# The last chunk of a feature-interaction network done by halves of its columns in two accumulators

**The chip, the cores and the metric.** One core of one Trainium2 chip. The time is that of the device, in microseconds (us), median of several executions.

## The reference

A batch of 1024 samples with 64 features of 16 numbers goes through three layers of a compressed interaction network:

```python
for i in range(n):                                   # n = 3
    z = einsum('bfe,bge->bfge', x0, h)               # all products of features
    y = einsum('oc,bce->boe', Ws[i], z) + bs[i][None, :, None]
    if i != n - 1: x_i, h = y[:, :64], y[:, 64:]     # half is kept, half goes on
    else: x_i = y
    xs.append(x_i)
pooled = sum(concatenate(xs, axis=1), axis=2)
return pooled @ fc_w.T + fc_b                        # one number a sample
```

## The kernel before

The batch is cut into 32 chunks of 512 columns (32 samples by 16 numbers). VectorE makes the products `z` of a chunk, TensorE contracts them with `w_all` in 16 matmuls into one accumulator of 128 x 512:

```python
def contract(c, j):
    for i in range(NI):                              # NI = NJ = 4
        t = j * NI + i
        nc.tensor.matmul(accs[c], w_all[:, t, w_cols(c)], zs[c, j][:, i, :], start=..., stop=...)
```

From chunk 8 on, four chunks make a group. Two kinds of small matmuls are shared by a group, in parts of the array that run side by side: the squares (32 rows of the array for each chunk), and for each pair of chunks two weighted matmuls and two `y` matmuls (a quarter of the array each):

```python
def contract_shared(first):
    for r in range(4):
        c, at = first + r, slice(32 * r, 32 * r + 32)
        nc.tensor.matmul(accs[c], w_sq[at, w_cols(c)], zls[first // 4][at], ..., tile_position=(32 * r, 0))
    for k in (first // 2, first // 2 + 1):
        ...
        for n in range(2):
            c, rows, q = 2 * k + n, halves[n], halves[1 - n]
            nc.tensor.matmul(accs[c][q], v1w[rows], xxs[k][rows], start=False, ...)
        for rows in halves:
            nc.tensor.matmul(ys[k][rows], bd[rows, rows], xxs[k][rows], start=True, stop=True)
```

Behind a chunk's last matmul come a copy on ScalarE and a multiply and a reduction on VectorE. The sums of all chunks are pooled by matmuls with a matrix of ones into `po`, and `finish` sends them out:

```python
def factors(c):
    ...
    nc.scalar.copy(q[h], accs[c][64 - h.start : 128 - h.start])
    nc.vector.scalar_tensor_tensor(uu, accs[c][h], bh1[h], q[h], ALU.add, ALU.mult)
...
# the end; chunk 31 has been contracted in the loop, with pool(first, 1), pool(first, 0)
# in its middle and finish(first) behind it (first: pairs 0 to 14, last: pair 15)
sums(NP - 1, parts=slice(1, 2))
sums(NP - 1, slice(0, 64), slice(0, 1))
pool(last, 1)
factors(NCH - 1)
sums(NP - 1, slice(64, 128), slice(0, 1))
pool(last, 0)
finish(last)
```

Of the kernel before, what the change touches and what calls it, by code (L numbers as in the profile page):

```python
# [32 lines left out]
F32 = mybir.dt.float32  # L36
AF = mybir.ActivationFunctionType
ALU = mybir.AluOpType
# [3 lines left out]
E = 16  # L42
B = 1024
CB = 32
N = CB * E
NCH = B // CB
NI = 4
NJ = 4
# [12 lines left out]
def cin_kernel(ctx, tc, xra, xrb, xh, wh, w0r, w1h, w2t, wx1, wx0, vec, out):  # L61
    nc = tc.nc
# [5 lines left out]
    sp = ctx.enter_context(tc.tile_pool(name="sp", bufs=2))  # L68
    ps = ctx.enter_context(tc.tile_pool(name="ps", bufs=2, space=bass.MemoryType.PSUM))
# [3 lines left out]
    def const_tile(name, shape):  # L73
        return const.tile(shape, F32, tag=name, name=name)

    def z_tile(name):

        return zp.tile([128, NI, N], F32, tag="z", name=name)

# [3 lines left out]
    def set_tile(name):  # L83
        return setup.tile([128, NI * N], F32, tag="set", name=name)

# [3 lines left out]
    fc2, bh1, bh2 = vs[:, 0:1], vs[:, 1:2], vs[0:64, 2:3]  # L89
# [18 lines left out]
    w_all = const_tile("w_all", [128, NT + 1, 192])  # L108
    w_sq = const_tile("w_sq", [128, 192])
    v1w = const_tile("v1w", [128, F])  # L110
# [5 lines left out]
    xas, xbs, zls, xxs = {}, {}, {}, {}  # L116

    def load_xa(c, at=slice(0, NI)):
        if c not in xas or at.start == 0:
            xas[c] = xp.tile([128, NI, N], F32, tag="xa", name=f"xa_{c}")  # L120
        nc.sync.dma_start(
            out=xas[c][:, at, :],
            in_=bass.AP(
                tensor=xra.tensor, offset=c * XR * N + at.start * N,
                ap=[[N, 128], [1, (at.stop - at.start) * N]],
            ),
        )

    def load_chunk(c):
        load_xa(c)  # L130
        xb = xp.tile([128, NJ, N], F32, tag="xb", name=f"xb_{c}")
        nc.sync.dma_start(out=xb, in_=xrb[c])
        xbs[c] = [xb[:, j, :] for j in range(NJ)]
# [20 lines left out]

    acc = const_tile("acc", [128, 2, NCH // 2, CB])
    hb = const_tile("hb", [128, NF, N // 2])
    accs, uus, zs, ys = {}, {}, {}, {}

    def new_acc(c, n=N):
        accs[c] = ps.tile([128, n], F32, tag="acc", name=f"acc_{c}", bufs=4)  # L160

    def product(c, j, pieces=1):
# [10 lines left out]
    def squares(c):  # L173
        zls[c] = xp.tile([128, N], F32, tag="zl", name=f"zl_{c}", bufs=4)
        nc.scalar.activation(zls[c][0:64], xas[c][0:64, 0, :], AF.Square)  # L175
# [16 lines left out]
    def w_cols(c):  # L192
        return slice(64, 192) if c >= FIRST and c % 2 else slice(0, 128)

    def contract(c, j):
        for i in range(NI):
            t = j * NI + i
            nc.tensor.matmul(  # L198
                accs[c], w_all[:, t, w_cols(c)], zs[c, j][:, i, :],
                start=(t == 0 and (c < FIRST or c % 4 < 2)),  # L200
                stop=(t == NT - 1 and c >= FIRST and c % 4 >= 2),
            )
# [4 lines left out]
    def contract_shared(first):  # L207

        for r in range(4):
            c, at = first + r, slice(32 * r, 32 * r + 32)  # L210
            nc.tensor.matmul(  # L211
                accs[c], w_sq[at, w_cols(c)], zls[first // 4][at], start=(r >= 2), stop=(r < 2),
                tile_position=(32 * r, 0),
            )
        for k in (first // 2, first // 2 + 1):
            ys[k] = ps.tile([128, N], F32, tag="y", name=f"y_{k}")
            for n in range(2):
                c, rows, q = 2 * k + n, halves[n], halves[1 - n]
                nc.tensor.matmul(  # L219
                    accs[c][q], v1w[rows], xxs[k][rows], start=False, stop=(c % 4 < 2),  # L220
                    skip_group_check=True,
                )
            for rows in halves:
                nc.tensor.matmul(ys[k][rows], bd[rows, rows], xxs[k][rows], start=True, stop=True)  # L224



    H2 = N // 2

    def half_contract(c, part, j):  # L230

# [2 lines left out]
        for t in (NT,) if j == NJ else range(j * NI, (j + 1) * NI):  # L234
            z = zls[c] if t == NT else zs[c, j][:, t % NI, :]
            for n in range(2):
                nc.tensor.matmul(  # L237
                    accs[c][halves[n]], w_all[rows, t, cols], z[rows, n * H2 : (n + 1) * H2],
                    start=(t == 0), stop=(t == NT),
# [5 lines left out]
    def uu_tile(k):  # L245
        if k not in uus:
            uus[k] = sp.tile([128, 2, N], F32, tag="uu", name=f"uu_{k}")
        return uus[k]

    def factors(c):  # L250

        uu = uu_tile(c // 2)[halves[c % 2], 0, :]
        if c in HEAD:
            for n in range(2):
                at = halves[n]
                nc.vector.tensor_tensor(  # L256
                    uu[:, n * H2 : (n + 1) * H2], accs[c][at], hb[at, HEAD.index(c), :], ALU.mult
                )
            return
        h = halves[c % 2 if c >= FIRST else 0]  # L260
        q = sp.tile([128, N], F32, tag="q", name=f"q_{c}")
        nc.scalar.copy(q[h], accs[c][64 - h.start : 128 - h.start])  # L262
        nc.vector.scalar_tensor_tensor(uu, accs[c][h], bh1[h], q[h], ALU.add, ALU.mult)  # L263

    def v0x(k):
        ys[k] = ps.tile([128, N], F32, tag="y", name=f"y_{k}")
# [2 lines left out]
    def x_v0x(k):  # L269
        nc.vector.scalar_tensor_tensor(uu_tile(k)[:, 1, :], ys[k], cx, xxs[k], ALU.add, ALU.mult)  # L270

    def sums(k, rows=slice(0, 128), parts=slice(0, 2)):

        nc.vector.tensor_reduce(  # L274
            acc[rows, parts, k, :],
            uus[k][rows, parts].rearrange("p k (b e) -> p k b e", e=E),
            AX.X,
            ALU.add,
        )
# [5 lines left out]


    new_acc(c0, H2)
    squares(c0)
    for j in range(NJ):
# [14 lines left out]
    for n in range(2):  # L304
        pv = ps.tile([128, 512], F32, tag="set", name=f"pv2_{n}")
        for k in range(4):
            nc.tensor.matmul(
                pv[32 * k : 32 * k + 32], fv2, w2s[n][:, k * 512 : (k + 1) * 512],
                start=True, stop=True,
                tile_position=(0, 32 * k),  # L310
            )
        nc.scalar.copy(v2r[:, n, :], pv)


    new_acc(c1, H2)
    for j in range(NJ - 1):
        product(c1, j)
# [56 lines left out]
    def head(c):  # L374
        new_acc(c, H2)
        for j in range(NJ):
            product(c, j)
        for j in range(NJ + 1):
            half_contract(c, 0, j)
        keep_h1(c)  # L380
# [29 lines left out]

    new_acc(c4, H2)
    for j in range(NJ - 1):
# [52 lines left out]
    for j in range(2):  # L465
        nc.tensor.matmul(
            pc, fcol[:, j : j + 1].to_broadcast([128, 2]), bcol[:, j : j + 1],
            start=(j == 0), stop=(j == 1),
# [13 lines left out]

    NP = NCH // 2
    po = ps.tile([2, NP, CB], F32, tag="set", name="po")
# [3 lines left out]
    def pool(pairs, part):  # L488
        nc.tensor.matmul(  # L489
            po[:, pairs, :], ones, acc[:, part, pairs, :],  # L490
            start=(part == 1), stop=(part == 0), skip_group_check=True,
        )

    def finish(pairs):
        nc.scalar.activation(res[:, pairs, :], po[:, pairs, :], AF.Identity, bias=cst)  # L495
        nc.scalar.dma_start(out=outs[:, pairs, :], in_=res[:, pairs, :])


    order = list(range(2, NCH))
    first, last = slice(0, NP - 1), slice(NP - 1, NP)  # L500
    for s, c in enumerate(order):
        k, shared = c // 2, c >= FIRST
        if s + 2 < len(order):
            ahead = order[s + 2]
            load_chunk(ahead)
            last_tile(ahead)
            for j in range(NJ):
                product(ahead, j)
        if not shared or c % 4 < 2:
            new_acc(c, H2 if c in HEAD else N)  # L510
        for j in range(NJ):
            if j == 2:
                if s == 0:
                    for n in KEPT:
                        half_contract(n, 1, NJ)
                if s == 1:
                    v0x(0)
                if c % 2 and not shared:
                    v0x(k)
                if s == len(order) - 1:  # L520
                    pool(first, 1)
                    pool(first, 0)
            if c in HEAD:
                half_contract(c, 1, j)
            else:
                contract(c, j)
        if c in HEAD:
            half_contract(c, 1, NJ)
        elif not shared:
            contract_last(c)  # L530
        elif c % 4 == 1:
            for n in (1, 2):
                new_acc(c + n)
            contract_shared(c - 1)
        if s == len(order) - 1:
            finish(first)

        if s == 0:
            for n in KEPT:
                factors(n)  # L540
        elif not shared or c % 4 in (0, 3):
            factors(order[s - 1])
        elif c % 4 == 2:
            factors(c - 2)
            factors(c - 1)
            x_v0x(k - 1)
            x_v0x(k)
        if s == 1:
            x_v0x(0)
            sums(0)  # L550
        if c % 2 and not shared:
            x_v0x(k)
        elif s and c % 2 == 0:
            sums(k - 1)
    sums(NP - 1, parts=slice(1, 2))
    sums(NP - 1, slice(0, 64), slice(0, 1))
    pool(last, 1)
    factors(NCH - 1)
    sums(NP - 1, slice(64, 128), slice(0, 1))
    pool(last, 0)  # L560
    finish(last)

# [71 lines left out]
```

## Time and profile before

| | before |
|---|---|
| time | 501.08 us median of 6 runs, 500.87 to 501.39 |
| TensorE's share of the chain that ended last | 91% |
| from the last group's squares to the end | 37.48 us |
| a group's squares, weighted and `y` matmuls | 2.948 us, in each of the six groups |
| copy, multiply, reduction behind the last matmul | 0.577, 0.757, 0.682 us |

TensorE is busy without a gap from early on, so whatever lengthens its stream lengthens the kernel; only behind the last matmul do the other engines set the time. The lines stand in the prediction.

### The profile page before, as it was taken

To read this page: it belongs to the slowest core of one execution; us is meant where nothing else is said; L and a number is where in the kernel's file an instruction comes from. 1 tells how busy PE (TensorE), PEld (TensorE's weight loads), DVE (VectorE), ACT (ScalarE), POOL (GpSimd) and SP (SyncE) were. 2 spreads that over 40 slices of the span, in tenths; PEclk is the share of its full clock that TensorE was granted. 3 is DMA by queue.
4 is the path that set the end of the run, shared out by engine and by line. 5 is a ranking of instruction groups with operands and counts; after the bars stand their busy time and mean duration, and the time that the engine had idled before them with its cause. 6 is when DMAs were issued, how large, how long until landed. Compare 5 with 4: busy or idle time off the path is not lost.

```text
span 499.2 us, 4338 instructions
## 1 busy us (share of the span) xinstructions
PE 483.8 (97%) x1814; PEld 222.6 (45%) x1814; DVE 381.8 (76%) x233; ACT 92.5 (19%) x159; POOL 1.4 (0%) x14
## 2 busy tenths in 40 slices
PE   3899999999999999999999999999999999999996
PEld 1455654456444344443444434443444434444432
DVE  4999699988999889898777686776877777770302
ACT  1243033122111121312011121111111121010001
POOL 1000000000000000000000000000000000000000
PEclk9999999999999999999999999999999999999999
DMA  8997895353454443446144442333444430000000
GB/s 327 425 419 226 338 421 208 116 230 129 181 235 175 170 174 162 177 175 256 66 169 169 168 168 113 118 136 138 168 169 168 167 131 39 0 0 0 2 0 0
DMA packets 14787, 82.80 MB, mean 166 GB/s; under 512 B 3788, under 2 KB 4460, under 8 KB 5232
## 3 DMA queue, kind: packets, MB, share of 16 engines
q1 hardware_dynamic: 13644, 81.24, 41.5%
q10 hardware_dynamic: 1124, 1.29, 0.9%
q8 instruction: 14, 0.23, 0.2%
q14 instruction: 5, 0.04, 0.0%
HBM read 80.88 MB, written 1.64 MB: 165 GB/s over the span
## 4 chain that ended last, share of the span: by engine, by line
PE 91%; DMA 5%; ACT 1%; ACTq 0%; SPq 0%; DVE 0%; issue 0%
PE acc L198 75%; PE acc L237 11%; DMA w1s<-in_w1h 4%; PE acc L219 2%; DMA xb<-in_xrb 1%; PE acc L211 1%; PE y L267 1%; PE acc L205 1%; PE pm L336 0%; PE po L489 0%; ACT zl L175 0%; ACT zl L181 0%; ACT m_sb L341 0%; ACT xx L190 0%; ACTq L360 0%
## 5 line engine op out<-in xcount | busy, mean ns | idle before, releaser
L198 PE MATMUL acc<-z,w_all 128*128 128x512 f32 x864 | 374.1, 593 | 0.0
L166 DVE TENSOR_TENSOR z<-xa,xb 128x2048 f32<-128x2048 f32 (+1 forms) x141 | 314.9, 2270 | 49.9 <-PE acc L198 39.7
L198 PEld LDWEIGHTS acc<-z,w_all 128*128 128x128 f32 x864 | 163.3, 190 | 208.3 <-issue 207.8
L237 PE MATMUL acc<-z,w_all 128*64 128x256 f32 x640 | 74.7, 389 | 10.4 <-DVE w_all L282 8.4
L171 ACT ACTIVATE z<-xa 32x512 f32<-32x512 f32 x35 | 21.9, 625 | 323.5 <-DVE z L166 320.7
L263 DVE SCALAR_TENSOR_TENSOR uu<-acc,vs,q 64x512 f32<-64x512 f32 x27 | 20.2, 750 | 62.4 <-ACT q L262 62.3
L237 PEld LDWEIGHTS acc<-z,w_all 128*64 128x64 f32 x640 | 45.8, 140 | 39.1 <-DVE w_all L282 9.9
L274 DVE TENSOR_REDUCE acc<-uu 128x64 f32<-128x1024 f32 (+2 forms) x18 | 20.2, 1125 | 0.3
L190 ACT COPY xx<-xa 64x512 f32<-64x512 f32 x32 | 19.6, 613 | 0.4
L262 ACT COPY q<-acc 64x512 f32<-64x512 f32 x27 | 15.7, 580 | 19.3 <-PE y L224 12.9
L186 ACT ACTIVATE sq<-xa 32x512 f32<-32x512 f32 x24 | 15.1, 628 | 0.6
L270 DVE SCALAR_TENSOR_TENSOR uu<-y,cx,xx 128x512 f32<-128x512 f32 x16 | 11.4, 745 | 0.3
L224 PE MATMUL y<-xx,bd 64*64 64x512 f32 x48 | 11.6, 602 | 0.0
L219 PE MATMUL acc<-xx,v1w 64*64 64x512 f32 x48 | 11.6, 602 | 0.0
L211 PE MATMUL acc<-sq,w_sq 32*128 32x512 f32 x48 | 6.8, 640 | 0.0
L175 ACT ACTIVATE zl<-xa 64x512 f32<-64x512 f32 x11 | 6.8, 623 | 0.1
L219 PEld LDWEIGHTS acc<-xx,v1w 64*64 64x64 f32 x48 | 2.8, 132 | 7.9 <-issue 7.9
L237 PE MATMUL acc<-zl,w_all 64*64 64x256 f32 (+1 forms) x40 | 6.1, 393 | 0.0
L243 ACT ACTIVATE hb<-acc,vs 128x256 f32<-128x256 f32 x5 | 2.4, 474 | 20.0 <-PE acc L237 20.0
L495 ACT ACTIVATE res<-po,cst 2x480 f32<-2x480 f32 (+1 forms) x2 | 0.9, 464 | 24.0 <-PE po L489 24.0
L181 ACT COPY zl<-xa 64x512 f32<-64x512 f32 x8 | 4.9, 616 | 0.1
L256 DVE TENSOR_TENSOR uu<-acc,hb 64x256 f32<-64x256 f32 x10 | 4.2, 421 | 0.2
(52 smaller groups left out, 52.0 us busy)
## 6 DMA issues: line engine op xcount, KB each, us to landing
xa<-in_xra SPq DMA_DIRECT2D x34, 1024.0 KB, 4.8
xb<-in_xrb SPq DMA_DIRECT2D x34, 1024.0 KB, 7.0
w<-in_w2t SPq DMA_DIRECT2D x2, 1024.0 KB, 13.5
xa<-in_xra SPq DMA_DIRECT2D x2, 512.0 KB, 4.1
w1s<-in_w1h SPq DMA_DIRECT2D x1, 1024.0 KB, 20.3
w1x<-in_wx SPq DMA_DIRECT2D x1, 1024.0 KB, 8.7
w0x<-in_wx SPq DMA_DIRECT2D x1, 1024.0 KB, 10.3
xb<-in_xrb SPq DMA_DIRECT2D x1, 768.0 KB, 7.0
```

Of the source, the lines that this page charges most:

```text
L166: nc.vector.tensor_tensor(zs[c, j][:, i : i + n, :], xas[c][:, i : i + n, :], xbs[c][j].unsqueeze(1).to_broadcast([128, n, N]), ALU.mult,)
L171: nc.scalar.activation(zs[c, j][SQ, 0, :], xas[c][SQ, 0, :], AF.Square)
L186: nc.scalar.activation(zls[c // 4][at : at + 32], xas[c][0:32, 0, :], AF.Square)
L190: nc.scalar.copy(xxs[c // 2][to], xas[c][to, 0, :])
L198: nc.tensor.matmul(accs[c], w_all[:, t, w_cols(c)], zs[c, j][:, i, :], start=(t == 0 and (c < FIRST or c % 4 < 2)), stop=(t == NT - 1 and ...
L211: nc.tensor.matmul(accs[c], w_sq[at, w_cols(c)], zls[first // 4][at], start=(r >= 2), stop=(r < 2), tile_position=(32 * r, 0),)
L219: nc.tensor.matmul(accs[c][q], v1w[rows], xxs[k][rows], start=False, stop=(c % 4 < 2), skip_group_check=True,)
L224: nc.tensor.matmul(ys[k][rows], bd[rows, rows], xxs[k][rows], start=True, stop=True)
L237: nc.tensor.matmul(accs[c][halves[n]], w_all[rows, t, cols], z[rows, n * H2 : (n + 1) * H2], start=(t == 0), stop=(t == NT),)
L262: nc.scalar.copy(q[h], accs[c][64 - h.start : 128 - h.start])
L263: nc.vector.scalar_tensor_tensor(uu, accs[c][h], bh1[h], q[h], ALU.add, ALU.mult)
L274: nc.vector.tensor_reduce(acc[rows, parts, k, :], uus[k][rows, parts].rearrange("p k (b e) -> p k b e", e=E), AX.X, ALU.add,)
```

## The change

The intent: contract the last chunk's first 256 columns completely, then the second 256 into another accumulator. The first half's copy, multiply and reduction run while TensorE does the second half, and only steps of 256 columns are left behind the last matmul. The core of the diff:

```diff
     def new_acc(c, n=N):
+        if c == NCH - 1:
+            parts[c] = [
+                (ps.tile([128, H2], F32, tag=tag, name=f"acc_{c}_{n}", bufs=bufs), cols)
+                for n, (tag, bufs, cols) in enumerate(
+                    (("acc", 4, slice(0, H2)), ("set", 2, slice(H2, N)))
+                )
+            ]
+            return
... contract, the squares, the weighted matmuls and factors go over the parts of chunk 31 ...
-                if s == len(order) - 1:
-                    pool(first, 1)
-                    pool(first, 0)
...
-        if s == len(order) - 1:
-            finish(first)
...
-    sums(NP - 1, parts=slice(1, 2))
+    sums(NP - 1, of=slice(1, 2))
     sums(NP - 1, slice(0, 64), slice(0, 1))
-    pool(last, 1)
     factors(NCH - 1)
-    sums(NP - 1, slice(64, 128), slice(0, 1))
+    sums(NP - 1, slice(64, 128), slice(0, 1), slice(0, CB // 2))
+    for j in range(NJ):
+        if j == 2:
+            pool(first, 1)
+            pool(first, 0)
+            pool(last, 1)
+        contract(NCH - 1, j, 1)
+    finish(first)
+    factors(NCH - 1, slice(1, 2))
+    sums(NP - 1, slice(64, 128), slice(0, 1), slice(CB // 2, CB))
     pool(last, 0)
     finish(last)
```

More of the change, by code (lines that the diff above doesn't have):

```diff
@@ L45 @@
 N = CB * E
+H2 = N // 2
 NCH = B // CB
@@ L156, in cin_kernel @@
     hb = const_tile("hb", [128, NF, N // 2])
-    accs, uus, zs, ys = {}, {}, {}, {}
+    accs, uus, zs, ys, parts = {}, {}, {}, {}, {}
     def new_acc(c, n=N):
+        if c == NCH - 1:
[6 more added lines that the diff above has]
+            return
         accs[c] = ps.tile([128, n], F32, tag="acc", name=f"acc_{c}", bufs=4)
@@ L193, in w_cols, with pieces, contract @@
         return slice(64, 192) if c >= FIRST and c % 2 else slice(0, 128)
-    def contract(c, j):
+    def pieces(c):
+        return parts[c] if c in parts else [(accs[c], slice(0, N))]
+    def contract(c, j, piece=0):
+        acc_c, cols = pieces(c)[piece]
         for i in range(NI):
@@ L198, in contract @@
             nc.tensor.matmul(
-                accs[c], w_all[:, t, w_cols(c)], zs[c, j][:, i, :],
+                acc_c, w_all[:, t, w_cols(c)], zs[c, j][:, i, cols],
                 start=(t == 0 and (c < FIRST or c % 4 < 2)),
@@ L210, in contract_shared @@
             c, at = first + r, slice(32 * r, 32 * r + 32)
-            nc.tensor.matmul(
-                accs[c], w_sq[at, w_cols(c)], zls[first // 4][at], start=(r >= 2), stop=(r < 2),
-                tile_position=(32 * r, 0),
-            )
+            for acc_c, cols in pieces(c):
+                nc.tensor.matmul(
+                    acc_c, w_sq[at, w_cols(c)], zls[first // 4][at, cols], start=(r >= 2),
+                    stop=(r < 2), tile_position=(32 * r, 0),
+                )
         for k in (first // 2, first // 2 + 1):
@@ L218, in contract_shared @@
                 c, rows, q = 2 * k + n, halves[n], halves[1 - n]
-                nc.tensor.matmul(
-                    accs[c][q], v1w[rows], xxs[k][rows], start=False, stop=(c % 4 < 2),
-                    skip_group_check=True,
-                )
+                for acc_c, cols in pieces(c):
+                    nc.tensor.matmul(
+                        acc_c[q], v1w[rows], xxs[k][rows, cols], start=False, stop=(c % 4 < 2),
+                        skip_group_check=True,
+                    )
             for rows in halves:
                 nc.tensor.matmul(ys[k][rows], bd[rows, rows], xxs[k][rows], start=True, stop=True)
-    H2 = N // 2
     def half_contract(c, part, j):
@@ L248, in uu_tile, with factors @@
         return uus[k]
-    def factors(c):
+    def factors(c, which=slice(0, 1)):
         uu = uu_tile(c // 2)[halves[c % 2], 0, :]
@@ L260, in factors @@
         h = halves[c % 2 if c >= FIRST else 0]
-        q = sp.tile([128, N], F32, tag="q", name=f"q_{c}")
-        nc.scalar.copy(q[h], accs[c][64 - h.start : 128 - h.start])
-        nc.vector.scalar_tensor_tensor(uu, accs[c][h], bh1[h], q[h], ALU.add, ALU.mult)
+        for acc_c, cols in pieces(c)[which]:
+            q = sp.tile([128, N], F32, tag="q", name=f"q_{c}_{cols.start}")
+            nc.scalar.copy(q[h, cols], acc_c[64 - h.start : 128 - h.start])
+            nc.vector.scalar_tensor_tensor(
+                uu[:, cols], acc_c[h], bh1[h], q[h, cols], ALU.add, ALU.mult
+            )
     def v0x(k):
@@ L270, in x_v0x, with sums @@
         nc.vector.scalar_tensor_tensor(uu_tile(k)[:, 1, :], ys[k], cx, xxs[k], ALU.add, ALU.mult)
-    def sums(k, rows=slice(0, 128), parts=slice(0, 2)):
+    def sums(k, rows=slice(0, 128), of=slice(0, 2), half=slice(0, CB)):
         nc.vector.tensor_reduce(
-            acc[rows, parts, k, :],
-            uus[k][rows, parts].rearrange("p k (b e) -> p k b e", e=E),
+            acc[rows, of, k, half],
+            uus[k][rows, of, E * half.start : E * half.stop].rearrange("p k (b e) -> p k b e", e=E),
             AX.X,
```

## The prediction

> **What bounds the kernel now.** I read the page first, parts 1, 2 and 4, to see which engine sets the end; then the chain of work over the last 40 us, to see the order of the end; then the groups by form for the durations; then the engines' own timelines around the places that the change touches.
>
> ```profile
> PE 483.8 (97%) x1814; PEld 222.6 (45%) x1814; DVE 381.8 (76%) x233; ACT 92.5 (19%) x159; POOL 1.4 (0%) x14
> PE   3899999999999999999999999999999999999996
> DVE  4999699988999889898777686776877777770302
> PE 91%; DMA 5%; ACT 1%; ACTq 0%; SPq 0%; DVE 0%; issue 0%
> ```
>
> TensorE is the bound: 91% of the chain that ended last, nines from the third slice to the last but one. Nothing that takes time from VectorE or ScalarE matters except behind the last matmul. The chain there:
>
> ```profile
> 464.78 20.80 PE acc L198 x48
> 485.58 1.70 PE po L489 x4
> 487.28 7.08 PE acc L198 x16
> 494.36 0.02 issue
> 494.38 0.58 ACT q L262
> 494.97 0.03 issue
> 494.99 0.77 DVE uu L263
> 495.76 0.02 issue
> 495.79 0.69 DVE acc L274
> 496.48 0.04 issue
> 496.52 0.23 PE po L489 x2
> 496.76 0.02 issue
> 496.78 0.28 ACT res L495
> ```
>
> One matmul of the program is two instructions in the trace (432 calls of L198 in the code, x864 on the page), so chunk 31 is 32 instructions of 512 columns, split 16 and 16 by the pooling of the first 15 pairs. Behind it stand six steps, 494.36 to 497.06, then the output's DMA (to 499.2). Three of the six, the copy, the multiply and the reduction, have 512 columns: 0.58 + 0.77 + 0.69 = 2.04 us. These are what the change halves. The rest (final pooling, 32-column activation, DMA) has no 512.
>
> The places where the change adds matmuls:
>
> ```profile
> 461.76 1.14 PE L211 MATMUL acc<-sq,w_sq 32*128 32x512 f32 x8
> 462.84 0.65 PE L219 MATMUL acc<-xx,v1w 64*64 64x512 f32 x2
> 462.85 0.65 PE L224 MATMUL y<-xx,bd 64*64 64x512 f32 x2
> 463.32 0.59 PE L219 MATMUL acc<-xx,v1w 64*64 64x512 f32 x2
> 463.33 0.60 PE L224 MATMUL y<-xx,bd 64*64 64x512 f32 x2
> ```
>
> Here several matmuls run at once in different parts of the array: the four calls of one pair (two of L219, two of L224) start together as first passes at 462.84, and their second passes start together 0.48 us later. The trace shows such grouping only where the calls use different parts; the pairs of L237, which come back to the same two parts, run pair by pair, 0.21 us a step.
>
> **What the Trainium skill says.**
> - "TensorE: Matmul & The Clock Gate", Back-to-back issue gap: the warm gap is the columns over the rate plus about 2.5 ns fixed. The trace has the same shape at half that rate: 429 ns for 512 columns (427 at 1.2 columns a ns, and 2). The L237 pairs of 256 columns repeat every 215 to 216 ns. So two of 256 cost about 2 ns more than one of 512.
> - Same page, LDWEIGHTS: a load takes the columns over 1.2, here 107 ns, and can be pulled ahead under the running matmul. The trace agrees: two exposed loads start 108 ns apart; each is recorded as 190 ns and starts 2 ns after the matmul before. 190 is under 213, so under a 256-column matmul it should still be hidden. No 256-column matmul with 128 weight columns is in this trace.
> - Same page, The mechanism: matmuls start in order. It matters below, where a second half needs a part of the array that the first half still uses.
> - "TensorEngine Tiling (Array Packing)", Key Properties: changing the tiling mode drains the array. The trace agrees: going into the pooling the step is 523 ns and not 429, and the first step coming back is 534, so 0.20 us for the round trip. The change keeps one such trip.
>
> **The change part by part.**
> 1. Behind the last matmul. Copy: ScalarE's slope here is (651 - 278) / 448 = 0.83 ns a column (480 and 32 columns of L495); 256 columns fewer are 0.21 us, leaving 0.37. Multiply: VectorE's slope is (1224 - 420) / 768 = 1.05 ns a column (L166 and L282 forms); 0.27 us fewer, leaving 0.49. Reduction: (1215 - 669) / 512 = 1.07; 0.27 us fewer, leaving 0.41. Sum: -0.75 us, all on the path.
> 2. The contraction of chunk 31: 64 instructions of about 215.6 ns = 13.80 us against 32 x 428.9 = 13.72: +0.07 us on the path.
> 3. The last pair's first pooling (two 32-column instructions, 28 ns apart at 494.28) moves from beside the ScalarE copy into the stream: +0.06 us. The first pairs' pooling (1.70 us) only moves from between two quarters to between two eighths: 0.
> 4. The squares' matmul of chunk 31 (L211, its fourth row part) becomes two. The other three parts run their second pass of 427 ns while the fourth does 213, so its second half can start in the free half of that time: its two passes of 213 then end 213 + 213 + 213 = 640 ns after the second passes' start instead of 427, less what goes before the mode switch's drain; taking the load into account I put +0.1 to +0.3 us, middle 0.2.
> 5. The weighted matmul of chunk 31 (L219) becomes two in one part. If the group breaks where a part comes back, the five calls run as {30, 31a} and {31b, y, y}: 31a's second pass ends at 640 ns, then 31b, y and y start, and y's two passes of 427 end at 1494 instead of 854: +0.64 us. If all first passes go before all second passes, in order, y starts behind 31a at 213: +0.21 us. If the parts ran wholly on their own: 0. I take +0.35.
> 6. The output of the first 15 pairs goes from 487.3 to about 490.8 on ScalarE (0.65 us and 0.50 of issue), 3 us before the last copy: 0. The copy of chunk 30, which waited for it until 488.55, moves to about 478.6: nothing waits for it.
> 7. The first half's copy, multiply and reduction run under the second half's matmuls: 485.3 to about 486.7, and the pooling wants them at 488.7 at the earliest: 0.
>
> Sum: -0.75 + 0.07 + 0.06 + 0.2 + 0.35 = -0.07 us; span 499.1, time 501.0. The gain and what it costs are of one size.
>
> **The rivals.**
> - The clean gain: the added matmuls of 4 and 5 fit into the array's free parts. For it: the parts do run side by side (four within 20 ns of each other). Against: starts are in order, and a second half returns to a busy part. It makes -0.75 + 0.13 = -0.62, 500.5 us.
> - The groups break: 4 and 5 at their worst, 0.3 + 0.64. For it: the L237 pairs never mix with the next pair. It makes +0.3, 501.4 us.
> - The weight loads no longer hide under 213 ns. For it: the record says 190 and 23 ns remain; PEld is then nearly always busy. Against: what the array needs is 107. If 20 ns showed on each of 64, +1.3 us: 501.7 to 502.3. I give it one in ten.
> - A wait takes the place: the final pooling or the second accumulator waits. Against: the second accumulator takes a bank whose last user (a constant's set-up) is long done by chunk 8, and the first 15 pairs' output ran at once after its pooling in the kernel before, though later matmuls had been issued, so its wait is exact. A late first output would cost up to 1.2 us; one in twenty.
>
> **Range and chances.** All outcomes worked out lie between 500.5 and 502.3, within 0.3% of 501.09; the three runs of before span 0.2. The likely mass is 500.4 to 501.5. 2% is 10 us, the whole tail behind the last matmul is 5 us, so neither side of 2% has a mechanism.
>
> **What would show it right or wrong.** The chain's end should read about 0.37, 0.49, 0.41 for copy, multiply and reduction; larger values fell step 1. 32 instructions of L198's line with 256 columns should take 6.9 us; 7.5 or more would mean exposed loads (step 2). From the start of the fourth group of squares to the start of chunk 30's contraction the kernel before takes 464.71 - 461.76 = 2.95 us; after, 2.95 would show the clean gain, 3.5 my middle, 3.9 broken groups (steps 4 and 5). An idle stretch of TensorE before the pooling, or the long ScalarE activation behind 494, would show a new wait.

## The result

The changed kernel takes 500.51 us (median of 6 runs, 500.32 to 500.66); before, 501.08. That is 0.57 us less. Ratios are the mean time of one kernel's fast runs over that of the other's of the same rounds, so not quite the ratio of the medians: 0.9989, with a 95% interval of 0.9976 to 1.0001, which just includes 1: the whole time alone does not settle that there is a gain, and the rest rests on the traces.

From the page of the changed kernel, the busy line and the shares of the chain that ended last:

```profile
PE 483.2 (97%) x1850; PEld 229.3 (46%) x1850; DVE 382.3 (77%) x235; ACT 92.7 (19%) x160; POOL 1.4 (0%) x14
PE 91%; DMA 5%; ACT 1%; SPq 0%; ACTq 0%; issue 0%; DVE 0%
```

The bound is the same: TensorE has 91% of the chain. 36 matmul instructions were added: 32 in the contraction, two in the squares and two in the weighted matmuls. The end of the chain that ended last, after (start, duration, what):

```profile
488.98 1.76 PE po L507 x6
490.74 3.67 PE acc L213 x16
...
494.43 0.37 ACT q L278
...
494.82 0.50 DVE uu L279
...
495.35 0.43 DVE acc L292
495.78 0.14 issue
495.91 0.23 PE po L507 x2
```

The three steps read 0.37, 0.50 and 0.43 where they read 0.58, 0.77 and 0.69. One line is new: between the reduction's end and the last pooling there is 0.14 us of "issue" where there was 0.04. (By the single times of the trace, used from here on, the gap is 0.147 us and was 0.056.)

The place where I had expected half the gain to be lost, TensorE's timeline over the last group's weighted and `y` matmuls (start, duration, engine, line, operation, tiles, shapes, count):

```profile
463.60 0.59 PE L236 MATMUL acc<-xx,v1w 64*64 64x512 f32 x2
463.61 0.65 PE L241 MATMUL y<-xx,bd 64*64 64x512 f32 x2
463.82 0.80 PE L236 MATMUL acc<-xx,v1w 64*64 64x256 f32 x3
464.09 0.60 PE L241 MATMUL y<-xx,bd 64*64 64x512 f32 x2
464.25 0.38 PE L236 MATMUL acc<-xx,v1w 64*64 64x256 f32 x1
464.62 0.70 PE L213 MATMUL acc<-z,w_all 128*128 128x512 f32 x1
```

L236 is the weighted matmul, L241 is `y`. The program issues chunk 30's weighted matmul, the two halves of chunk 31's, and then the two `y`. Single starts in the trace: chunk 31's part starts a 256-column pass at 463.606, 463.822, 464.038 and 464.253, every 0.216 us without a gap; the first passes of both `y` start at 463.613 and 463.619, before the second half of chunk 31, which stands ahead of them in the program. The whole group takes 3.004 us instead of 2.948. Almost all of that is in `y`, not in chunk 31's part. Before, the weights of this pair's `y` were loaded while the first pair's matmuls still ran (from 463.331, the matmul at 463.758). Now they are loaded only at 463.610 and 463.617, with the matmuls, and from first to second pass it takes 0.480 us instead of 0.429.

Where the time went, both traces from the start of the last group's squares to the end, 37.483 us before and 37.017 after:

| term | us |
|---|---|
| copy 0.577 to 0.363, multiply 0.757 to 0.491, reduction 0.682 to 0.416 | -0.746 |
| the group's squares (1.071 to 1.076) | +0.005 |
| the group's weighted and `y` matmuls (1.877 to 1.928) | +0.051 |
| the contraction of chunks 30 and 31 (27.932 to 28.012, pooling taken out) | +0.080 |
| pooling in the stream (1.701 to 1.760) | +0.059 |
| from the reduction's end to the last pooling's start (0.056 to 0.147) | +0.091 |
| the rest | -0.006 |
| sum | -0.466 |

The span of the two profiled runs differs by 0.617 us. The other 0.15 lie before the first group's squares (171.37 us into the trace before, 171.22 after), where the two programs are the same. The same changed kernel, run once more in a later job (a set of runs on one chip), began them at 172.05. This part is not the change's.

### The profile page after: what moved, and what is told of

It reads as the page before. It is cut to its first block, busy times and chain, and to the rows that moved or that the text cites. A ratio compares the mean times of both kernels' runs of the same rounds, so it can differ in the third digit from the quotient of the medians.

```text
span 498.6 us, 4414 instructions
## 1 busy us (share of the span) xinstructions
PE 483.2 (97%) x1850; PEld 229.3 (46%) x1850; DVE 382.3 (77%) x235; ACT 92.7 (19%) x160; POOL 1.4 (0%) x14
## 4 chain that ended last, share of the span: by engine, by line
PE 91%; DMA 5%; ACT 1%; SPq 0%; ACTq 0%; issue 0%; DVE 0%
PE acc L213 75%; PE acc L252 11%; DMA w1s<-in_w1h 4%; PE acc L236 2%; DMA xb<-in_xrb 1%; PE acc L227 1%; PE y L285 1%; PE acc L220 1%; PE po L507 0%; PE pm L354 0%; ACT zl L185 0%; ACT zl L191 0%; ACT m_sb L359 0%; ACT xx L200 0%; ACTq L378 0%
## 5 line engine op out<-in xcount | busy, mean ns | idle before, releaser
L213 PE MATMUL acc<-z,w_all 128*128 128x512 f32 (+1 forms) x896 | 374.2, 578 | 0.0
L213 PEld LDWEIGHTS acc<-z,w_all 128*128 128x128 f32 x896 | 169.4, 190 | 202.1 <-issue 200.0
L279 DVE SCALAR_TENSOR_TENSOR uu<-acc,vs,q 64x512 f32<-64x512 f32 (+1 forms) x28 | 20.5, 731 | 61.5 <-ACT q L278 61.3
L278 ACT COPY q<-acc 64x512 f32<-64x512 f32 (+1 forms) x28 | 15.8, 564 | 36.4 <-PE acc L213 22.9
L292 DVE TENSOR_REDUCE acc<-uu 128x64 f32<-128x1024 f32 (+3 forms) x19 | 20.3, 1073 | 0.4
L241 PE MATMUL y<-xx,bd 64*64 64x512 f32 x48 | 11.7, 604 | 0.0
L236 PE MATMUL acc<-xx,v1w 64*64 64x512 f32 (+1 forms) x50 | 11.6, 584 | 0.0
L227 PE MATMUL acc<-sq,w_sq 32*128 32x512 f32 (+1 forms) x50 | 6.8, 620 | 0.0
L236 PEld LDWEIGHTS acc<-xx,v1w 64*64 64x64 f32 x50 | 3.1, 132 | 7.5 <-issue 7.4
L227 PEld LDWEIGHTS acc<-sq,w_sq 32*128 32x128 f32 x50 | 2.2, 183 | 4.6 <-issue 4.5
```

Of the source, the lines that this page charges most:

```text
L213: nc.tensor.matmul(acc_c, w_all[:, t, w_cols(c)], zs[c, j][:, i, cols], start=(t == 0 and (c < FIRST or c % 4 < 2)), stop=(t == NT - 1 and ...
L227: nc.tensor.matmul(acc_c, w_sq[at, w_cols(c)], zls[first // 4][at, cols], start=(r >= 2), stop=(r < 2), tile_position=(32 * r, 0),)
L236: nc.tensor.matmul(acc_c[q], v1w[rows], xxs[k][rows, cols], start=False, stop=(c % 4 < 2), skip_group_check=True,)
L278: nc.scalar.copy(q[h, cols], acc_c[64 - h.start : 128 - h.start])
L279: nc.vector.scalar_tensor_tensor(uu[:, cols], acc_c[h], bh1[h], q[h, cols], ALU.add, ALU.mult)
L292: nc.vector.tensor_reduce(acc[rows, of, k, half], uus[k][rows, of, E * half.start : E * half.stop].rearrange("p k (b e) -> p k b e", e=E), ...
```

## The experiments

The open points: why the halves in the shared matmuls cost almost nothing; whether the gain is that of the tail (the steps behind the last matmul) alone; where the new 0.09 us in front of the last pooling come from; and how far the cut could go. "Stretch" below is the time from the start of the last group's squares to the end of the trace; it is 37.483 us for the kernel before and 37.017 for the changed one. Twelve kernels ran.

**The pooling behind the last matmul.**

```diff
             pool(first, 0)
-            pool(last, 1)
         contract(NCH - 1, j, 1)
     finish(first)
+    pool(last, 1)
```

> The change, with the last pair's first pooling moved from the middle of the second half's matmuls to behind the last one, after the output of the first 15 pairs. Theory (a second wait): in the changed kernel the last pooling is the first writer of that accumulator after ScalarE has read it, so it waits for ScalarE as well as for VectorE, and TensorE spends an extra 51 ns event instruction behind the reduction (gap from the reduction's end to the matmul 147 ns, 56 before the change). With the other pooling taking the wait for ScalarE while the tail's copy runs, the gap should go back to about 56 ns, and the two 32-column matmuls (0.06 us) leave the stream: 0.15 us less than the change, 500.36 by the clock of the changed kernel's 500.51. Rival (the gap comes from somewhere else, the chip's state or the shorter reduction): the gap stays near 147 ns and only 0.06 us goes, 500.45.

Measured: 500.39 us against 501.02 of the kernel before in the same rounds (ratio 0.9987, interval 0.9974 to 0.9999); stretch 36.872, which is 0.145 less than the change. The pooling in the stream is back to 1.70 us. The chain of waits at the end:

```profile
495.27 0.43 DVE acc L292
495.69 0.04 issue
495.74 0.23 PE po L507 x2
```

The gap is back to 0.054 us (0.04 on the chain). The theory of a second wait holds, the rival falls.

**The last pair's pooling in a bank of its own.**

```diff
+    pos = {0: po}
     def pool(pairs, part):
+        if pairs.start not in pos:
+            pos[pairs.start] = ps.tile([2, 1, CB], F32, tag="y", name="po_last")
         nc.tensor.matmul(
-            po[:, pairs, :], ones, acc[:, part, pairs, :], ...
+            po_of(pairs), ones, acc[:, part, pairs, :], ...      # finish reads po_of(pairs) too
```

> The change, with the last pair's two poolings in a bank of their own, at the same places in the program. Theory (a second wait): nothing of the last pooling's accumulator is read by ScalarE before, so only the wait for VectorE is left: gap from reduction to matmul about 56 ns, no event instruction on TensorE there, the pooling in the stream still 1.76 us; 0.09 us less than the change, 500.42. Rival (the gap belongs to the shorter reduction or to chance): gap about 147 ns, 500.51.

Measured: stretch 36.921, so 0.096 less than the change, with the pooling in the stream still 1.76 us and the gap 0.054. The end of its chain:

```profile
496.00 0.04 issue
496.04 0.23 PE po_last L514 x2
```

The time, 500.54, doesn't show it: in its profiled run the last group began 0.22 us later than in the changed kernel's, in a part of the program that is the same. The trace settles it, the time does not. Where the event instruction sits on TensorE's sequencer, from the view of the pooling's line: first the kernel before, then the changed one (count, duration in ns, start in us).

```profile
L489 PEldq EVENT_SEMAPHORE  x1: 51/51/51, 490.5 to 490.5; - x1
```

```profile
L507 PEldq EVENT_SEMAPHORE  x1: 51/51/51, 495.8 to 495.8; - x1
```

It is the same instruction in both, for a pooling that waits for VectorE and for ScalarE. Before, `pool(last, 1)` carried both waits, at 490.5, while TensorE had matmuls queued. In the change `pool(last, 1)` comes before `finish(first)`, so `pool(last, 0)` is the first to write `po` after ScalarE has read it, and the two waits come at 495.8, behind the reduction, on the path. The semaphores that the traces give for the last pooling say the same: VectorE's alone in the kernel before, VectorE's on the event instruction and ScalarE's on the pooling in the change.

**Halves in one accumulator, the tail whole.**

```diff
-            nc.tensor.matmul(accs[c], w_all[:, t, w_cols(c)], zs[c, j][:, i, :], ...)
+            w = N // 2 if c == NCH - 1 else N
+            for n in range(0, N, w):
+                nc.tensor.matmul(accs[c][:, n : n + w], w_all[:, t, w_cols(c)], zs[c, j][:, i, n : n + w], ...)
```

> The kernel before, with the last chunk's contraction in pairs of 256-column matmuls into one accumulator; the squares and the weighted matmuls stay whole and the steps behind the last matmul keep 512 columns. Theory: the halves cost only the fixed 2 to 3 ns of each matmul, a step of 215.7 ns instead of 429 for two, so +0.08 us on the kernel before, 501.16, and no gain at all, because the gain is the tail's. Rival A (weight loads show under 213 ns): steps of 235 ns or more, +0.7 us or more. Rival B (narrower matmuls let the end come earlier in themselves): below 501.0. In this order each weight is loaded twice in a row, so the number of loads is that of the change.

Measured: 501.03 us against 501.02, stretch 37.556, +0.073 on the kernel before; steps of 215 to 216 ns. No gain without the shorter tail, and no weight load that shows at 256 columns, which rules out the prediction's third rival.

**Only the tail in halves, whole matmuls.**

```diff
-    factors(NCH - 1)
-    sums(NP - 1, slice(64, 128), slice(0, 1))
+    for n in range(2):
+        factors_half(NCH - 1, n)                     # copy and multiply of 256 columns
+    for n in range(2):
+        sums(NP - 1, slice(64, 128), slice(0, 1), slice(n * CB // 2, (n + 1) * CB // 2))
```

> The kernel before, with whole matmuls, and only the steps behind the last one done in halves: copy, copy on ScalarE, multiply, multiply, reduce, reduce on VectorE, each with 256 columns. Theory (the gain is that the first half's steps run beside the second half's matmuls): no gain here, since all six come behind the last matmul; by the changed kernel's durations 0.36 + 0.03 + 2 x 0.49 + 2 x 0.42 = 2.2 us from the copy's start to the last reduction's end, 2.08 before: +0.1 us, 501.1. Rival (two engines side by side on smaller pieces give the gain by themselves): 1.7 us or less there, 500.7 or below.

Measured: 501.78 us against 501.58 (ratio 1.0004, unclear at this size), stretch 37.858, +0.375. From the copy's start to the last reduction's end it took 2.468 us, 2.084 before. The direction is the theory's, the size is not: ScalarE's timeline shows why.

```profile
494.23 0.36 ACT L255 COPY q<-acc 64x256 f32<-64x256 f32 x1 [5.26 <-PE acc L198]
495.15 0.36 ACT L255 COPY q<-acc 64x256 f32<-64x256 f32 x1 [0.56 <-DVE uu L256]
```

The second copy waited 0.56 us for the first multiply, which reads the same accumulator. The wait is written in the program: built again, it has the second copy wait for the first multiply, and the two have no other buffer in common. So the tool that builds the program puts two engines' readings of one accumulator in order, and the run does not show what the engines could do. The two halves did not run side by side at all. This run shows no gain from smaller steps alone, but with one accumulator; it does not say what two would give behind whole matmuls.

**The shared matmuls in halves, in all six groups.**

```diff
+            w = N // 2 if r == 3 else N                       # squares of the fourth chunk
+            for i in range(0, N, w): ... accs[c][:, i : i + w] ...
...
+                w = N // 2 if c % 4 == 3 else N               # its weighted matmul
+                for i in range(0, N, w): ... accs[c][q, i : i + w] ...
```

> The kernel before, with the squares and the weighted matmul of the odd chunk of the second pair in two halves of 256 columns, as the change does for chunk 31, but in all six groups of four chunks, and in one accumulator. Six times what steps 4 and 5 of the prediction speak of. Own parts (each part of the array works off its own matmuls, whatever the others do): about 0.05 us a group as the changed kernel's trace shows, +0.3 us, 501.3. All first passes before all second ones, in order: about 0.4 us a group, +2.5, 503.5. Broken groups: about 0.85 us a group, +5.1, 506.1.

Measured: each of the six groups takes 3.003 to 3.004 us, 0.055 more than before, 0.33 in all; 501.89 us against 501.58 of the same rounds (ratio 1.0002, unclear at this size). "Own parts" holds; first passes in order (0.4 us a group) and broken groups (0.85) both fall.

**The same, the halves first in the program.**

```diff
-        for r in range(4):
+        for r in (3, 0, 1, 2):
...
-            for n in range(2):
+            for n in (1, 0):
```

> As e4_shared_six, but with those halves first in the program within their squares and within their pair, so that everything else comes behind a second half that must wait for its part. Own parts: no difference from e4_shared_six within 0.1 us a group, about 501.3. Starts in the order of the program: the other parts can't begin before the second half begins, 0.21 us (first passes together) to 0.43 us later, for the squares and for the pair each: +2.5 to +5.1 us on the kernel before.

Measured: groups of 3.005 to 3.006 us, 502.08 us against 501.58 (ratio 1.0009, interval 0.9996 to 1.0023). The order of the program costs 0.002 us a group at most. TensorE's timeline of the last pair, L223 weighted, L228 `y`:

```profile
465.19 0.65 PE L223 MATMUL acc<-xx,v1w 64*64 64x256 f32 x2
465.21 0.65 PE L228 MATMUL y<-xx,bd 64*64 64x512 f32 x2
465.41 0.86 PE L223 MATMUL acc<-xx,v1w 64*64 64x256 f32 x3
465.69 0.60 PE L228 MATMUL y<-xx,bd 64*64 64x512 f32 x2
```

Both `y` start 0.02 us after the first half, though the second half, which the program has ahead of them, can't start for another 0.2. One rival is that the tool that builds the program had put the `y` ahead; it had not: built again, this kernel has both halves, the other weighted matmul and the two `y` on TensorE's list in that order.

**One extra matmul in each of two parts, and both in one part.** Results are wrong on purpose.

```diff
-                nc.tensor.matmul(accs[c][q], v1w[rows], xxs[k][rows], ...)
+                for _ in range(2 if c % 4 in (0, 3) else 1):  # e7c_same_part: (1, 3)
+                  nc.tensor.matmul(accs[c][q], v1w[rows], xxs[k][rows], ...)
```

> The kernel before, wrong result on purpose: the weighted matmul is issued twice for the first chunk of a group (in one part of the array) and for the fourth (in another part). A matmul of two passes of 512 columns takes a part 0.86 us. Own parts that run ahead of one another across the two pairs of a group: each of the two parts has three matmuls instead of two, one unit more, +0.86 us a group, +5.1 us in six groups, 506.2. Pairs that wait for one another: the first pair takes two units and the second takes two, two units more, +1.7 us a group, +10.3, 511.3. Results wrong on purpose (the weighted terms of those chunks count twice).

> Control of e7_two_parts, wrong result on purpose: the same two extra weighted matmuls a group, but both in one part of the array (second and fourth chunk of a group). If the longest part sets the group's time: four matmuls of 0.86 us in that part instead of two, 1.72 us more a group than 2.95, so 4.67 to 4.75 (e7_two_parts: 3.84). If the number of extra matmuls counted, or pairs waited for one another, this and e7_two_parts would be the same.

Measured: with the extra ones in two parts a group takes 3.843 us, +0.895; both in one part 4.652, +1.704. The first took 506.50 us against 501.58; the second was run once, so its state is unknown, with 511.93 us against 501.25, and it is the groups in its trace that count here. TensorE's timeline of the first one's last group, L220 weighted, L225 `y`:

```profile
468.70 0.65 PE L220 MATMUL acc<-xx,v1w 64*64 64x512 f32 x2
468.72 0.65 PE L225 MATMUL y<-xx,bd 64*64 64x512 f32 x2
469.13 0.65 PE L220 MATMUL acc<-xx,v1w 64*64 64x512 f32 x2
469.20 0.60 PE L225 MATMUL y<-xx,bd 64*64 64x512 f32 x2
469.56 1.07 PE L220 MATMUL acc<-xx,v1w 64*64 64x512 f32 x4
```

The second pair's `y` (468.72 and 469.20) run beside weighted matmuls that the first pair still owes, and the third matmul of each of the two parts ends side by side in the last row, two passes of two parts. So pairs don't wait for each other: three units of 0.86 us in the fullest part instead of two, where waiting pairs would have taken four. The number of extra matmuls is the same in both kernels; what sets a group's time here is the part with the most work.

**The cut at 384 and 128, and at 448 and 64 columns.**

```diff
-    (("acc", 4, slice(0, H2)), ("set", 2, slice(H2, N)))
+    (("acc", 4, slice(0, CUT)), ("set", 2, slice(CUT, N)))     # CUT = 384, 448; sums cut at CUT // E
```

> The change, cut at 384 and 128 columns instead of 256 and 256. The three steps behind the last matmul lose another 128 columns: 0.11 + 0.13 + 0.13 = -0.37 us against the change. The matmuls of 128 columns need 107 ns of streaming[...]. Theory (a load needs 107 ns of the array and hides): steps of about 109 to 115 ns, so about +0 to +0.2 us for the 32 instructions; total 500.15 to 500.35. Rival (the recorded 190 ns of a load must pass before its matmul starts): steps of about 190 ns, +2.6 us, total 502.7. In the change the rival could not be seen, since 190 is under 213.

> The change, cut at 448 and 64 columns, to see what a weight load of 128 columns takes of the array when the matmul is too narrow to cover it. The 64-column matmul streams for 53 ns. Theory (a load takes 107 ns of the array, and the next can begin only when the matmul before has begun): steps of 107 to 112 ns, the same as with 128 columns, so the contraction of the chunk is 32 x (376 + 111) = 15.6 us against 13.8 of the change, +1.8, the tail -0.57: about 1.2 us slower than the change, from the squares to the end 38.2. Rival (loads are no limit, 128 columns took 112 ns for another reason): steps of about 56 ns, no loss, 36.5.

Measured at 384: 500.23 us against 501.02 (ratio 0.9983, interval 0.9971 to 0.9996), stretch 36.722, 0.295 less than the change; the tail from copy to reduction's end 0.965 us (1.338 in the change), the steps of 128 columns 112 ns. At 448: 502.07 against 501.25 (ratio 1.0015, interval 1.0002 to 1.0029), stretch 38.179; the tail 0.777, but the steps of 64 columns take 112 ns too. The last 16 instructions, on TensorE's timeline of the one and of the other:

```profile
492.52 2.05 PE L214 MATMUL acc<-z,w_all 128*128 128x128 f32 x16
```

```profile
494.50 2.00 PE L214 MATMUL acc<-z,w_all 128*128 128x64 f32 x16
```

Half the columns, the same time: here the columns no longer set the step. That the weight loads do, and not a fixed price of an instruction, is seen in the kernel before: with 64 weight columns and 4 moving ones (its line 324) the matmuls of one part repeat every 58 ns, and the poolings with 2 weight columns and 32 moving ones every 28. The recorded 190 ns of a load do not count, else 128 columns would have taken 190; two loads that no matmul hides start 108 ns apart in the kernel before.

**Both improvements together.**

```diff
+ CUT = 384, and pool(last, 1) behind finish(first)
```

> Both improvements of the change together: cut at 384 and 128 columns, and the last pair's first pooling behind the last matmul. From the start of the last group's squares to the end, the kernel before takes 37.48 us, the change 37.02, the cut alone 36.72, the moved pooling alone 36.87. If the two gains add: 36.57, so 0.91 us less than before and 0.45 less than the change; about 0.1% faster than the change of the same job. If the wait for ScalarE comes back at the shorter tail (ScalarE's copy is 0.11 us shorter): 36.66.

Measured: 500.44 us, in the same rounds as the change once more and the kernel before: 501.24 and 501.25 (ratio to before 0.9984, interval 0.9972 to 0.9997). Stretch 36.572: the gains add. By the stretch this version beats both kernels; by the time it beats the kernel before (no interval was made against the change).

**The change once more.**

> The changed kernel itself once more, for comparison within this job: 37.02 us from the start of the last group's squares to the end, 3.00 us of it the group; about 0.1% faster than the kernel before.

Measured: stretch 37.015, group 3.003, as in its first profile. But its median in these rounds, 501.24 (500.79 to 501.28), is that of the kernel before, 501.25 (500.87 to 502.00); ratio 0.9994, interval 0.9981 to 1.0008. So "about 0.1% faster" missed. The part of the program before the first group's squares, which no run changes, varies by more than the change gains: over all profiles it ended between 171.20 and 172.52 us.

## Why the prediction was right, and which step was off

The range held, and that the time would stay within 2% was right; the middle, 501.0, was 0.5 us too slow. That the time lay in the range says little of the mechanism, since the range held the clean gain (500.5) and the broken groups (501.4) alike, and a quarter of the profiled difference (0.15 of 0.617 us) is not the change's: so far the close fit to 500.5 is luck. The group's 3.00 us in the trace decides between them. What was measured is close to what the prediction called the clean gain, plus a wait that it had not counted.

- Step 1, -0.75: -0.746 measured. The slopes per column from other groups of the same profile were enough for three durations that the trace did not have.
- Step 2, +0.07: +0.080. The steps are 216 ns as taken from the L237 pairs. That the loads hide at 256 columns was argued from 190 under 213; the cut at 128 showed that 190 was the wrong number to compare and about 112 the right one (under its rivals the prediction had set 107 against it).
- Step 3, +0.06: +0.059.
- Step 4, "+0.1 to +0.3 us, middle 0.2": +0.005. Step 5, "I take +0.35": +0.051. These two terms, 0.55 us together and 0.056 measured, are what put the middle too high; the second wait of step 6 took 0.09 of it back. The step that failed is that "matmuls start in order", so that a second half holds up what comes behind it. In its place the runs show that each part of the array works off its own matmuls: the time is unchanged with the halves first in the program (3.006), and goes with the longest part (3.843 against 4.652). Chunk 31's part has the same 1024 columns to stream for two passes as the others, only cut in four, one every 0.216 us. The 0.051 us left are the weights of `y`, loaded only once chunk 31's first half had begun; why, no run shows.
- Step 6, "0": the output itself costs nothing, but moving the pooling in front of it put a second wait on the last pooling, +0.091 measured. The rival "a wait takes the place" named the final pooling, but argued only that the output's wait is exact. I had followed the waits of ScalarE for TensorE, not those of TensorE for ScalarE.
- The prediction counts six steps behind the last matmul; its lines show five (copy, multiply, reduction, pooling, activation) and the output's DMA. Nothing hangs on it.
- Step 7, 0: right. The first half's reduction ended at 486.90, the pooling began at 488.91.

The mark set beforehand, 2.95 us for the clean gain, 3.5 for the middle, 3.9 for broken groups, read 3.00.

## What to carry to other kernels

When the steps behind the last matmul are long, cut the last piece so that most of its columns finish early; the smaller end piece may shrink until the matmul is about as short as its weight load (of the three cuts tried, an end of 128 columns beat 256, and 64 lost to both). Small matmuls in separate parts of the array could be counted part by part here, and the fullest part set the time (0.895 and 1.704 us more for one and two further matmuls of 0.86). When work is moved, ask for each buffer who now writes it first after another engine has read it: that instruction gets the extra wait, and it should not be the one at the very end.

## What the Trainium skill lacked or had wrong

- "TensorE: Matmul & The Clock Gate", The mechanism, has matmuls start strictly in the order of the program. Here matmuls of other parts of the array started ahead of earlier ones whose part was busy: both `y` of the last pair at 463.61 and 463.62, chunk 31's second half, earlier in the program, not before 463.82, where its part of the array is free at the earliest. The order of the program made next to no difference (3.003 and 3.006 us). How far one part may run ahead of another no page says; "TensorEngine Tiling (Array Packing)", Key Properties, only has tiles operate independently.
- "TensorE: Matmul & The Clock Gate", LDWEIGHTS, gives the load's length but no floor for the step of fp32 load and matmul, and the spacing of such pairs under Back-to-back issue gap names no type: 112 ns for 128 weight columns, the same with 128 and 64 moving columns, and 216 ns at 256, where the load hides.
- No page that I read gives the price of a second wait on a TensorE instruction: an event instruction of 51 ns, and 91 ns more on the path.
